# A two-layer graph network: attention steps of three, three and two tiles of keys, each bank of scores with its own tile and activation

## The chip, the cores and the metric

The kernel runs on one core of a Trainium2 chip, as one launch. The metric is the device time of that core in microseconds, as the median of several runs. All data are float32. The core has five engines that run side by side and wait for each other through semaphores: TensorE (PE, matrix products), VectorE (DVE), ScalarE (ACT), GpSimd (POOL) and SyncE (SP, which here only issues DMAs). TensorE writes its results to PSUM, which has eight banks; a bank holds 512 float32 numbers in each of 128 partitions.

## The reference

Sixteen graphs (B) of 1024 nodes (N) with 256 features (C) go through two layers. Layer 0 normalizes, makes queries by a weighted graph product, keys and values by a dense product, and attends with four heads of 64 features. Layer 1 normalizes again, aggregates over the graph and applies two dense products with batch norms. Cut to what bears on the change:

```python
h = jnp.maximum(_layernorm(x), 0.0)
# layer 0
c_adj = jnp.mean(fea, axis=1)                     # fea: h, features first
A = |sigmoid(c_m - c_n) - 0.5| - 0.5, made symmetric, weights adj
g = relu(einsum('bcn,bnm->bcm', fea, Wg) * para)
q = g, split into 4 heads of 64
k, v = (h @ kv_w), split into 4 heads of 64
attn = softmax(einsum('bhnd,bhmd->bhnm', q, k) * scale, axis=-1)
x = x + einsum('bhnm,bhmd->bhnd', attn, v)
# layer 1
h = jnp.maximum(_layernorm(x), 0.0)
agg = einsum('nm,bmd->bnd', A_hat, h)             # A_hat from adj and its degrees
h1 = relu(batchnorm(agg @ W1.T + b1))
x = x + batchnorm(h1 @ W2.T + b2)
```

(The line for `A` and the splits are written out in words here; `...` of the module's other parts are left away.)

## The kernel before, in words

**Units and steps.** Attention is cut into 64 units: a graph b, a pair of heads k (two heads, 128 features together) and a half f of the queries (512 of them). A unit goes over 8 tiles of 128 keys. It is done in steps of two tiles, so four steps a unit, 256 steps in all, 16 a graph. `attention()` (L1215) is the loop over the steps; all instructions of a step are issued in this order:

1. `scores()` (L1043): for each of its tiles, matmuls of keys with queries for both heads (`e`), into a PSUM tile `sc` of two banks, one bank a head; each matmul is split in two halves of 64 keys, so that the four matmuls of a tile lie on four quarters (64*64) of TensorE's array. Then one activation `Exp` on ScalarE over both banks (128 x 1024) makes the tile `p` (L1064). The pool `ps_sc` has two such PSUM tiles, four banks in all; `p` comes from the pool `p4` with four buffers.
2. Actions that were put down for the top or the middle of this step: the sums, the gather and the finish of earlier units.
3. `Unit.add()` (L1079): VectorE adds the step's `p` tiles into `acc`, for the sum over the keys (L1085, L1088).
4. `Unit.values()` (L1091): the values of the step *before*, products of its `p` tiles with v into the bank `o` (L1099, 128*64). After the unit's last step, `o` is transposed in squares to `os` and sent to memory (`out_d`, L1113 and L1117).
5. Pieces of the background, until their cost reaches what is due by this step.
6. Actions for the end of the step: the folds of a finished unit.

**The end of a unit.** Let s be the step in which a unit's last values are taken, which is the first step of the next unit. Its two folds (L1134 and L1135, one for each head: a transpose of `acc` in squares and a reduction to `part`) are issued at the ends of steps s and s+1. `sums` (L1139) stands in the middle of step s+3, right behind that step's scores: matmuls of `part` on TensorE (L1148), then three small VectorE operations that make the reciprocal `inv`. For the first unit of a graph (`opens`; not in graph 0) it is one step later. `gather` reads `os` back at the top of s+2, and `add_output` (L1182) multiplies and adds it to x in step s+4 (s+6 for `opens`).

**The background.** While graph b is attended, the other stages of its neighbours are fed between as pieces of about 1.7 us of TensorE work each: queries (`pg`), keys (`pk`) and values (`pv`) of graph b+1, the aggregation (`pa`) and the hidden layer (`py`) of graph b-1, and the norms and weights of graphs to come. `due` in `attention()` says how much is to be done by each step, evenly over a graph's steps; in the last graph it is bent a little. The products of all these pieces share the pool `ps_mm` of three banks; `o` has one bank, `sc` four, which is all of PSUM.

**Queues.** The schedule is written out by hand (`manual_schedule`): each engine takes its instructions in the order in which this program issues them, and the pools put in the waits for buffers.

**Other names that the change touches.** `rows` and the six columns in `deg` hold sums of the adjacency's rows, diagonals and columns, until graph() and degrees() have made `dinv`. `stats1` collects the statistics for the first batch norm. `csum` are the sums of the normalized features of a node; in `differences()` (L461) VectorE transposes them in squares into `turned`, and SP sends that to memory and reads it back as one row on all partitions (`cbc`), which ScalarE uses to make the weights. In this form `csum` lies in a tile `wide` of 32 columns whose last 24 POOL clears when the norm begins.

After attention of the last graph the second part (`second()`) runs the second dense product with its batch norms; the change does not touch it. A second build of the layers with `shifted_attention` stands behind a condition and is executed only where the first one left the range of the numbers; it is not executed with these inputs.

## Time and profile before

| | us |
|---|---|
| median of 3 runs | 2480.53 |
| lowest and highest | 2480.22, 2481.03 |
| the profiled execution | 2482.2 |
| its span, from the first to the last instruction | 2480.3 |
| TensorE busy | 2418.3 |
| VectorE busy | 1999.8 |
| ScalarE busy | 1261.2 |
| POOL busy | 565.2 |

The mean granted clock of TensorE is 0.992. The profile counts an engine as busy while at least one of its instructions is under way; matmuls overlap each other, so a busy TensorE need not be at its peak. In the lists of groups, a line has the source line, the engine, the operation, the tile written and the tiles read, the size, the count, then the busy time, the mean duration in ns of one, and the idle time of the engine before them with what ended it. In a timeline, a line has the start and the duration of a run of like instructions, and in brackets the idle time before them. PEld are the weight loads of TensorE. A float32 matmul shows as two records, so a step of two tiles has 16 records of scores and 8 of values.

In the steady middle (graphs 2 to 13) every graph repeats the pattern of the one before to within 0.1 us, 16 steps of 7.2 to 9.0 us.

### The profile page before, as it was taken

The page shows a single profiled execution, that of the slowest core. Times are in us where ns is not written, and L with a number is a line of the kernel's source. Part 1 is how long each engine was busy: PE and PEld are TensorE (multiplying, and loading weights), DVE is VectorE, ACT ScalarE, POOL GpSimd, SP SyncE. Part 2 cuts the span into 40 slices and gives each one's busy share as a digit, 9 for nine tenths or more (in the row PEclk, how much of TensorE's full clock was granted, in tenths as well). Part 3 has the DMA queues.
Part 4 walks back from the last instruction along what each step waited for, and adds up shares of the span by engine and source line. Part 5 has one row for each costly group of instructions (what it writes and reads, how often), then busy time and mean ns, then how long its engine had stood idle before and what let it go on. Part 6 is the DMA issues. An engine that isn't in the chain of part 4 may idle for free. (4 is left out here: it accounts for less than half of the span.)

```text
span 2480.3 us, 35952 instructions
## 1 busy us (share of the span) xinstructions
PE 2418.3 (97%) x13290; PEld 829.3 (33%) x13290; DVE 1999.8 (81%) x3103; ACT 1261.2 (51%) x1870; POOL 565.2 (23%) x632
## 2 busy tenths in 40 slices
PE   9999999999999999999999999999999999999995
PEld 4333232332323232323323232323233232334444
DVE  5678887979798888889797978888897978767775
ACT  7764454545463645545454645355454534345554
POOL 1480202112121202021111212120201102136652
PEclk9999999999999999999999999999999999999997
DMA  4665535354555544453545555544535453456559
GB/s 145 198 218 175 181 124 191 120 198 157 181 174 191 168 168 162 144 181 118 210 143 175 170 191 170 187 160 148 177 126 197 133 199 122 157 205 222 192 198 373
DMA packets 202682, 437.19 MB, mean 176 GB/s; under 512 B 21248, under 2 KB 96512, under 8 KB 196736
## 3 DMA queue, kind: packets, MB, share of 16 engines
q1 hardware_dynamic: 173328, 327.29, 39.9%
q0 software_dynamic: 29168, 107.50, 11.4%
q8 instruction: 107, 1.75, 0.3%
q14 instruction: 79, 0.65, 0.1%
HBM read 331.36 MB, written 103.35 MB: 175 GB/s over the span
## 5 line engine op out<-in xcount | busy, mean ns | idle before, releaser
L1064 ACT ACTIVATE p<-sc 128x1024 f32<-128x1024 f32 x512 | 495.6, 1020 | 581.4 <-PE sc L1056 579.7
L1088 DVE TENSOR_TENSOR acc<-acc,p 128x1024 f32<-128x1024 f32 x384 | 469.5, 1223 | 81.6 <-ACT p L1064 60.3
L1056 PE MATMUL sc<-q,k 64*64 64x512 f32 x4096 | 500.1, 603 | 4.2 <-ACT p L1064 4.2
L1099 PE MATMUL o<-p,v 128*64 128x512 f32 x2048 | 494.6, 604 | 0.0
L174 PE MATMUL pa<-aht,h_b 128*64 128x512 f32 x1536 | 346.0, 592 | 1.1 <-ACT h_b L368 1.1
L174 PE MATMUL pg<-w,x_h 128*64 128x512 f32 x1472 | 332.0, 592 | 1.9 <-DVE x_h L579 1.9
L1056 PEld LDWEIGHTS sc<-q,k 64*64 64x64 f32 x4096 | 131.7, 132 | 340.9 <-issue 287.8
L1117 POOL DMA_DIRECT2D out_d<-os x58 | 33.9, 584 | 914.9 <-DVE os L1113 883.9
L1099 PEld LDWEIGHTS o<-p,v 128*64 128x64 f32 x2048 | 124.4, 136 | 297.9 <-issue 272.4
L493 DVE SCALAR_TENSOR_TENSOR w<-w,adj 128x1024 f32<-128x1024 f32 x128 | 166.2, 1306 | 31.9 <-ACT w L514 26.1
L174 PEld LDWEIGHTS pa<-aht,h_b 128*64 128x64 f32 x1536 | 110.0, 137 | 220.7 <-issue 208.8
L174 PEld LDWEIGHTS pg<-w,x_h 128*64 128x64 f32 x1472 | 105.6, 137 | 212.4 <-issue 201.0
L506 ACT ACTIVATE w<-cbc,csum 128x512 f32<-128x512 f32 x256 | 170.3, 716 | 4.7 <-DMA cbc<-csum_d 4.7
L514 ACT ACTIVATE w<-w 128x1024 f32<-128x1024 f32 x128 | 135.5, 1059 | 2.5
L569 DVE TENSOR_TENSOR w<-w,w 128x1024 f32<-128x1024 f32 x112 | 133.2, 1219 | 1.5
L174 PE MATMUL py<-at,w1s 128*64 128x512 f32 x448 | 109.5, 598 | 9.7 <-DVE y L837 7.5
L174 PE MATMUL pv<-kvw_f,ht 128*64 128x256 f32 x1024 | 116.1, 379 | 0.0
L174 PE MATMUL pk<-ht,kvw_f 128*64 128x512 f32 x512 | 115.2, 592 | 0.2 <-ACT ht L430 0.2
L174 PE MATMUL py<-at,w 128*64 128x512 f32 x464 | 113.3, 595 | 1.3 <-DVE at L727 0.7
L368 ACT ACTIVATE x_h<-x_h,lnsm_a 128x256 f32<-128x256 f32 x120 | 70.5, 593 | 74.6 <-DMA aht<-aht_d 67.1
L1085 DVE TENSOR_TENSOR acc<-p,p 128x1024 f32<-128x1024 f32 x64 | 79.2, 1237 | 31.5 <-ACT p L1064 31.5
L1428 ACT ACTIVATE yin_f<-yin_f,sm_f 128x512 f32<-128x512 f32 x128 | 93.5, 802 | 15.0 <-DMA yin_f<-y_d 14.9
(197 smaller groups left out, 2967.1 us busy)
## 6 DMA issues: line engine op xcount, KB each, us to landing
aht<-aht_d SPq DMA_DIRECT2D x224, 512.0 KB
adj<-in_adj_dram SPq DMA_DIRECT2D x128, 512.0 KB
y_d<-y POOLq DMA_DIRECT2D x128, 256.0 KB, 3.8
yin_f<-y_d SPq DMA_DIRECT2D x32, 1024.0 KB
para<-in_para_dram SPq DMA_DIRECT2D x64, 256.0 KB
x_d<-x_x POOLq DMA_DIRECT2D x16, 1024.0 KB, 5.1
xo_f<-x_d SPq DMA_DIRECT2D x32, 512.0 KB
out_dram<-xo_f POOLq DMA_DIRECT2D x32, 512.0 KB, 11.1
```

The lines of the kernel that those rows point to most:

```text
L174: nc.tensor.matmul(dst[r], left[:, r], right, start=start, stop=stop)
L368: nc.scalar.activation(self.h[:, t, :], self.src[:, t, :], AF.Relu, bias=self.sm[:, 1, t : t + 1], scale=self.sm[:, 0, t : t + 1], accum_o ...
L493: nc.vector.scalar_tensor_tensor(w, w, 1.0, a, op0=ALU.add, op1=ALU.mult)
L506: nc.scalar.activation(w[:, t, :].rearrange("p (t q) -> p t q", q=P), cbc[:, q * NT // NH : (q + 1) * NT // NH], AF.Abs, bias=csum[:, th * ...
L514: nc.scalar.activation(made[i], made[i], AF.Tanh, scale=-0.5 / C)
L569: nc.vector.tensor_sub(block(i)[part], block(x)[part], block(y)[part])
L1056: nc.tensor.matmul(sc[part, e, :], ks[b][k][r, m * P + c * HW : m * P + (c + 1) * HW], qs[b][k][r, f * FB : (f + 1) * FB], start=True, sto ...
L1064: nc.scalar.activation(pr, sc, AF.Exp)
L1085: nc.vector.tensor_add(self.acc, self.held, pr)
L1088: nc.vector.tensor_add(self.acc, self.acc, pr)
L1099: nc.tensor.matmul(self.o[r, :], vs[b][k][:, m, r], pr[:, e, :], start=(m == 0), stop=(m == NT - 1),)
L1428: nc.scalar.activation(y, y, AF.Relu, bias=sh[:, j : j + 1], scale=scale[:, j : j + 1])
```

## The change

A step takes three, three and two tiles in place of two each (`GROUPS`), so a unit has three steps. A PSUM tile `sc` has one bank, of which there are four, and each gets an activation of its own (128 x 512). `p` gets six buffers. The sums come one step earlier as counted in steps (s+2, s+3 for `opens`), and the output is added at s+3 (s+5). The work due in the background is counted in tiles instead of steps. To make room, `rows` and five of the degree columns go into a part of `stats1` that is written late, and `csum` gets a tile of 8 columns; `turned` is filled by POOL and transposed in place.

```diff
+        p6 = attn.enter_context(tc.tile_pool(name=f"p6_{kind}", bufs=6, side="right"))
         ps_sc = attn.enter_context(
-            tc.tile_pool(name=f"ps_sc_{kind}", bufs=2, space=PSUM, side="right")
+            tc.tile_pool(name=f"ps_sc_{kind}", bufs=4, space=PSUM, side="right")
         )
...
-        rows = big.tile([P, NH, NT], F32, name="rows")
+        spare = stats1[:, HC - 1].rearrange("p a s -> p (a s)")[:, (B * NH - 10) * 6 :]
+        rows = spare[:, : NH * NT].rearrange("p (q t) -> p q t", t=NT)
...
-        deg_sm = big.tile([P, 6, NT], F32, name="deg")
+        dinv = big.tile([P, NT], F32, name="dinv")
         later = {}
-        row, diag, col, deg, tmp_deg, dinv = (deg_sm[:, i, :] for i in range(6))
+        row, diag, col, deg, tmp_deg = (
+            spare[:, (NH + i) * NT : (NH + i + 1) * NT] for i in range(5)
+        )
...
-                    wide = p2.tile([P, SQ], F32, tag="csum", name=f"csum_{b}")
-                    nc.gpsimd.memset(wide[:, NT:], 0.0)
-                    wides[b] = wide
-                    self.csum = csums[b] = wide[:, :NT]
+                    self.csum = csums[b] = p2.tile([P, NT], F32, tag="csum", name=f"csum_{b}")
...
             turned = p1.tile([P, SQ], F32, tag="csumt", name=f"csumt_{b}")
-            nc.vector.transpose(turned, wides[b])
+            nc.gpsimd.memset(turned[:, NT:], 0.0)
+            nc.gpsimd.tensor_copy(turned[:, :NT], csums[b])
+            nc.vector.transpose(turned, turned)
...
+        GROUPS = (0, 1, 2), (3, 4, 5), (6, 7)
...
-            for m in (2 * g, 2 * g + 1):
-                sc = ps_sc.tile([P, 2, FB], F32, tag="sc", name=f"sc_{b}_{k}_{f}_{m}")
+            for m in GROUPS[g]:
+                pr = p6.tile([P, 2, FB], F32, tag="p", name=f"p_{b}_{k}_{f}_{m}")
                 for e in range(2):
+                    sc = ps_sc.tile([P, FB], F32, tag="sc", name=f"sc_{b}_{k}_{f}_{m}_{e}")
                     r = slice(e * HD, (e + 1) * HD)
                     for c in range(2):
                         part = slice(c * HW, (c + 1) * HW)
                         nc.tensor.matmul(
-                            sc[part, e, :],
+                            sc[part, :],
                             ks[b][k][r, m * P + c * HW : m * P + (c + 1) * HW],
                             qs[b][k][r, f * FB : (f + 1) * FB],
                             start=True,
                             stop=True,
                         )
-                pr = p4.tile([P, 2, FB], F32, tag="p", name=f"p_{b}_{k}_{f}_{m}")
-                nc.scalar.activation(pr, sc, AF.Exp)
+                    nc.scalar.activation(pr[:, e, :], sc, AF.Exp)
                 made.append(pr)
...
-                for i, pr in enumerate(prs):
-                    m = 2 * g + i
+                for m, pr in zip(GROUPS[g], prs):
...
-                if g == NG - 1:
+                if g == len(GROUPS) - 1:
...
             units = [Unit(b, k, f) for b in range(B) for k in range(CC) for f in range(NH)]
+            NG = len(GROUPS)
...
-                    due = total * (s % per_graph + 1) / per_graph
+                    whole = CC * NH * NT
+                    past = (NH * unit.at[1] + unit.at[2]) * NT + GROUPS[g][-1] + 1
+                    due = total * past / whole
                     if b == B - 1:
-                        due -= 0.5 * min(s % per_graph + 1, (per_graph - 1 - s % per_graph) * 0.75)
+                        due -= 0.25 * min(past, (whole - past) * 0.75)
...
                             opens = last.by_squares and last.at[1:] == (0, 0)
-                            wait = 6 if opens else 4
-                            at_mid.setdefault(s + 3 + opens, []).append(last.sums)
+                            wait = 5 if opens else 3
+                            at_mid.setdefault(s + 2 + opens, []).append(last.sums)
```

The changed `shifted_attention` follows the same split into banks; it is not executed.

More of the change, by code (lines that the diff above doesn't have):

```diff
@@ L124, in layers @@
         invs = {}
-        csums, wides, cbcs, weighted, weighers, steps = {}, {}, {}, {}, {}, {}
+        csums, cbcs, weighted, weighers, steps = {}, {}, {}, {}, {}
         s1s = {}
@@ L1006, in shifted_attention @@
                     name = f"{b}_{hd}_{t}"
-                    sc = ps_sc.tile([P, N], F32, tag="sc", name=f"sc_{name}")
+                    scs = [
+                        ps_sc.tile([P, FB], F32, tag="sc", name=f"sc_{name}_{g}") for g in range(NH)
+                    ]
                     for g in range(NH):
                         nc.tensor.matmul(
-                            sc[:, g * FB : (g + 1) * FB],
+                            scs[g],
                             qs[b][k][r, t * P : (t + 1) * P],
@@ L1015, in shifted_attention @@
                         )
-                    sm = p2.tile([P, 3], F32, tag="smx", name=f"smx_{name}")
-                    nc.vector.tensor_reduce(sm[:, 0:1], sc, AX.X, ALU.max, negate=True)
-                    pr = p4.tile([P, N], F32, tag="p", name=f"p_{name}")
-                    nc.scalar.activation(
-                        pr, sc, AF.Exp, bias=sm[:, 0:1], accum_out=sm[:, 1:2]
-                    )
-                    nc.vector.reciprocal(sm[:, 2:3], sm[:, 1:2])
-                    pt = p4.tile([P, N], F32, tag="p", name=f"pt_{name}")
+                    sm = p2.tile([P, 6], F32, tag="smx", name=f"smx_{name}")
+                    for g in range(NH):
+                        nc.vector.tensor_reduce(sm[:, g : g + 1], scs[g], AX.X, ALU.max, negate=True)
+                    nc.vector.tensor_tensor(sm[:, 2:3], sm[:, 0:1], sm[:, 1:2], op=ALU.min)
+                    pr = p6.tile([P, N], F32, tag="p", name=f"p_{name}")
+                    for g in range(NH):
+                        nc.scalar.activation(
+                            pr[:, g * FB : (g + 1) * FB],
+                            scs[g],
+                            AF.Exp,
+                            bias=sm[:, 2:3],
+                            accum_out=sm[:, 3 + g : 4 + g],
+                        )
+                    nc.vector.tensor_add(sm[:, 5:6], sm[:, 3:4], sm[:, 4:5])
+                    nc.vector.reciprocal(sm[:, 2:3], sm[:, 5:6])
+                    pt = p6.tile([P, N], F32, tag="p", name=f"pt_{name}")
                     for g in range(NH):
```

## The prediction

> **What bounds the kernel now.** I read the page's busy table first, then the windows by stage, then the timeline of single attention steps, engine by engine, and last the waits.

> The page:

> ```profile
> span 2480.3 us, 35952 instructions
> PE 2418.3 (97%) x13290; PEld 829.3 (33%) x13290; DVE 1999.8 (81%) x3103; ACT 1261.2 (51%) x1870; POOL 565.2 (23%) x632
> L1064 ACT ACTIVATE p<-sc 128x1024 f32<-128x1024 f32 x512 | 495.6, 1020 | 581.4 <-PE sc L1056 579.7
> L1056 PE MATMUL sc<-q,k 64*64 64x512 f32 x4096 | 500.1, 603 | 4.2 <-ACT p L1064 4.2
> L1099 PE MATMUL o<-p,v 128*64 128x512 f32 x2048 | 494.6, 604 | 0.0
> ```

> TensorE is busy 97%, and in attention (about 54 to 2146 us) it hardly ever waits: 4.2 us in all before score matmuls. So a step costs what TensorE needs to issue it; ScalarE waits for TensorE (579.7 us), not the reverse. One step of TensorE, and its weight loads:

> ```profile
> 1008.45 1.95 PE L1056 MATMUL sc<-q,k 64*64 64x512 f32 x16
> 1010.33 0.31 PE L1148 MATMUL sums<-part,same 128*64 128x32 f32 x4
> 1010.47 1.92 PE L1099 MATMUL o<-p,v 128*64 128x512 f32 x8
> 1012.21 1.89 PE L174 MATMUL pg<-w,s_a 128*64 128x512 f32 x8
> 1013.93 1.89 PE L174 MATMUL pg<-w,x_h 128*64 128x512 f32 x8
> 1015.75 1.52 PE L1056 MATMUL sc<-q,k 64*64 64x512 f32 x12
> ...
> 1008.45 0.21 PEld L1056 LDWEIGHTS sc<-q,k 64*64 64x64 f32 x8 [0.81 <-issue]
> 1008.93 0.15 PEld L1056 LDWEIGHTS sc<-q,k 64*64 64x64 f32 x4 [0.28 <-issue]
> 1009.36 0.15 PEld L1056 LDWEIGHTS sc<-q,k 64*64 64x64 f32 x4 [0.28 <-issue]
> ```

> A tile of keys is 8 score records, in two waves of four side by side; a wave takes 0.429 us (the weight loads of the third wave come 0.43 after those of the second; the products from 1012.21 to 1015.75 are eight waves and one change of kind). The step from 1008.45 to 1015.75 is 7.30 us: 16 waves are 6.86, the sums 0.14, and 0.30 are left over. They lie where the array changes between 64*64 and 128*64 and in each kind's first wave.

> The start of attention shows the one place where two steps of scores follow each other with nothing between:

> ```profile
> 54.13 1.95 PE L1056 MATMUL sc<-q,k 64*64 64x512 f32 x16
> 56.57 2.00 PE L1056 MATMUL sc<-q,k 64*64 64x512 f32 x16 [0.49 <-ACT p L1064]
> ...
> 55.51 1.92 ACT L1064 ACTIVATE p<-sc 128x1024 f32<-128x1024 f32 x2
> ...
> 1009.61 1.94 ACT L1064 ACTIVATE p<-sc 128x1024 f32<-128x1024 f32 x2 [2.10 <-PE sc L1056]
> ```

> The third tile there waits until the first tile's activation (55.51 + 1.02) has emptied its banks. An activation that waits only for TensorE starts 1.16 us after its step (1009.61 against 1008.45).

> Last, VectorE around the second fold of a unit, in a step that starts at 1065.84:

> ```profile
> 1065.84 1.95 PE L1056 MATMUL sc<-q,k 64*64 64x512 f32 x16
> ...
> 1067.75 0.70 DVE L1134 STREAM_TRANSPOSE acc<-acc 128x512 f32<-128x512 f32 x1
> 1068.49 0.69 DVE L1135 TENSOR_REDUCE part<-acc 128x16 f32<-128x512 f32 x1
> ```

> The fold belongs to the end of the step before, and yet ends at 1069.18, 3.34 us into this one: VectorE runs that far behind TensorE. From the same times for every unit: in graphs 2 to 13 the second fold ends 6.6 us into step s+2 for a graph's first unit and 3.1 to 3.3 us for the other three (s is the step in which the unit's last values are taken). The sums today come one step later still, so nobody feels this.

> [...] last score wave to first values wave is 0.52 us instead of 0.43, the same into the scores. [...] here a tile's scores take 0.86 us and its activation 1.02. [...] so a score matmul that waits holds the values behind it; the 0.49 us at 56.57 is such a wait. [...] The trace's copies of 512 elements from PSUM take 585, and I use 585.

> **The change part by part.** The profiled run took 2482.2 us around its span of 2480.3; the median is 2480.5. Sums are made against the run, and 1.7 comes off at the end.

> (a) Steps go from 4 to 3 a unit, 64 units: 64 steps fewer, 0.30 each: **-19 us**. Matmuls, adds and background pieces keep their numbers.

> (b) The third tile of a step. There are four one-bank tiles for six banks of scores, so tile 3 takes the banks of tile 1 of the same step. Let a step start at 0. Tile 1's activations start at 1.15; the first head's ends at 1.73; the second starts 0.485 later (585 less the 0.10 overlap of today's pairs: 1.02 long, 0.92 apart), at 1.63, and ends at 2.22; 0.04 later (56.53 to 56.57) TensorE may go on, at 2.26. It would have come to tile 3 at 0.48 + 3 x 0.429 = 1.77. The first head is just in time, the second 0.49 late[...]. Two steps of three: 128 x 0.49 = **+63 us**. It is a new wait on TensorE; queued behind it are the values and the whole background of the step.

> (c) ScalarE late at such a step. Today the first activation of a step is later than 1.16 by 3.9 us a graph, unfelt: 0.7 at tile 2, 2.6 at tile 4, 0.5 at tile 14 in a steady graph (behind the tanh work of L506 and L514). The step that starts at tile 3 lies between the first two, about 1.7, and there it now stops TensorE in full. 14 graphs x 1.8 = **+25 us**; at least 0 (if the longer step lets ScalarE catch up), at most 3.9 x 14 = 55.

> (d) The sums come at s+2 instead of s+3 (s+3 for the first unit of a graph, from graph 1 on). For the other 48 units step s+2 is a unit's third, of two tiles: TensorE gets to the sums 1.87 us after its start, while `part` comes from the fold emitted at the end of s+1. With today's lag (1.0 to 4.6, graphs 0 and 15 included) TensorE waits 1.37 in the mean: 48 x 1.37 = **+66 us**. Behind this wait stand values and background again. Bounds: fold alone is 1.39 after the last background result, so 0.3 at least (+14); going through VectorE's list of a three-tile step by hand (three adds 3.9, weighing or hidden work up to 9, fold 1.4, against a step of 12.8 to 14) I get 2.6, 4.2 and 4.7 for the three units, mean wait 2.0 (+96).

> (e) At no cost: 1024 activations for 512 (0.97 us a tile instead of 0.92, 26 us in all on an engine that is half idle; beyond (b) and (c) covered by values and background). Six `p` buffers for three a step: still reused after two steps. The due times keep their totals. `rows` and the degree columns only move. The copy and memset of 8 and 24 columns on POOL in front of the transpose of the column sums: 15 times, some 0.5 us of VectorE wait each by POOL's small steps; the row is needed a step later (ScalarE's wait for it is 4.7 us in all today); if that cover fails, +7. The gather of `os` stays at s+2 and its use moves from s+4 to s+3, a step of 9 us or more away; it stands on SP behind the same loads as now, and if late it holds VectorE only.

> Sum: -19 + 63 + 25 + 66 = +135; 2482.2 + 135 - 1.7 = **2615 us**.

> **The rivals.**
> - Only the banks stop TensorE (b, c), the sums are in time because the 12.8 us step gives VectorE slack: 2480.5 + 69 = 2550. For it: VectorE is at 81%. Against it: the lag is made of work that follows the last background product, not of a backlog.
> - VectorE falls further behind in long steps: waits of 2.9 us at the sums (139), and the hidden stage, whose products wait for VectorE today already (7.5 us in all), loses 10 more: 2480.5 - 19 + 63 + 25 + 139 + 10 = 2698. For it: the hand count of 4.2 and 4.7. Against it: each stop of TensorE lets VectorE catch up.
> - Faster: tile 3 finds its banks empty, as one-bank activations are meant to allow, and (a) alone is left: 2461. It is one mechanism, the release of tile 1's second bank: it decides from a stall below 19/128 = 0.15 us a step, so the release would have to come at 1.92 instead of 2.26, and the fold within 1.9 us of its step. For it: the first head does fit (1.77). Against it: two activations in a row end no sooner than 1.15 + 1.07 by the trace.

> **How the numbers follow.** Forecast 0.61; sums in time 0.17; VectorE behind 0.15; faster 0.06; about equal 0.01. The range 2535 to 2690 takes in most of the second and third cases: (a) and (b) alone give 2524, the upper bounds of (c) and (d) 2675. About 0.2% is what a measurement of this kernel can tell from no change. Slower holds all but the last two cases: 0.93.

> **What would show it.** (a) right if the page has 192 steps with some 0.30 us left over each. (b) right if weight loads of scores wait for the activation some 128 times, and values follow 3.2 us after the start of a three-tile step and not 2.7; wrong if 2.7. (c): in each graph one such wait near 2 us. (d) right if the weight loads of the sums wait for the reduce, about 48 times by 1 to 2 us. TensorE's share should fall to some 94%, not more, since in (b) the first head's matmuls still run and count as busy. If TensorE's busy time falls with the steps and neither wait shows, I am wrong and it is faster.

## The result, and the profile after

| | before | after |
|---|---|---|
| median, us (4 runs each, side by side) | 2480.78 | 2701.72 |
| lowest and highest | 2480.22, 2484.66 | 2700.52, 2703.07 |
| after / before, 95% interval | | 1.0887 (1.0868 to 1.0906) |
| span of the profiled execution | 2480.3 | 2698.3 |
| mean granted TensorE clock | 0.992 | 0.974 |

The changed kernel is 221 us slower. The direction is the one forecast. The size is not: 2701.72 lies 87 us above the forecast of 2615 and outside its range. The page of the kernel after: busy times, two rows of the slices, and four groups.

```profile
span 2698.3 us, 36449 instructions
PE 2512.9 (93%) x13290; PEld 876.0 (32%) x13290; DVE 2012.9 (75%) x3103; ACT 1287.0 (48%) x2382; POOL 561.7 (21%) x646
...
PE   9958989899999999898999999998989999999995
...
PEclk9979999999999999999999999999999999999997
...
L1078 ACT ACTIVATE p<-sc 128x512 f32<-128x512 f32 x1024 | 520.9, 609 | 499.3 <-PE sc L1071 499.2
L1071 PE MATMUL sc<-q,k 64*64 64x512 f32 x4096 | 561.2, 606 | 42.1 <-ACT p L1078 41.8
L1112 PE MATMUL o<-p,v 128*64 128x512 f32 x2048 | 514.7, 636 | 0.0
...
L1161 PE MATMUL sums<-part,same 128*64 128x32 f32 x256 | 20.4, 236 | 92.6 <-DVE part L1148 92.6
```

TensorE, the bound before, has the same 13290 records and yet 94.6 us more of busy time (2512.9 against 2418.3): its matmuls wait with some of their tiles started, or run slower. The third slice (135 to 202 us) falls to 5 tenths, which no step of the forecast had foreseen. The waits of TensorE itself:

```profile
PE sums L1161 <- DVE part L1148: 92.6, 46, 6.1
PE sc L1071 <- ACT p L1078: 41.8, 18, 25.6
```

(total, times, longest.) The sums wait for the reduction of the fold 46 times. The scores wait only 18 times by this view, and 25.6 us of it is one wait; what the third tiles wait is hidden here, since the first head's matmuls still count as busy. The weight loads show it, in a three-tile step of the kernel after that starts at 1146.75:

```profile
1146.75 0.21 PEld L1071 LDWEIGHTS sc<-q,k 64*64 64x64 f32 x8 [0.81 <-issue]
1147.24 0.15 PEld L1071 LDWEIGHTS sc<-q,k 64*64 64x64 f32 x4 [0.28 <-issue]
1147.67 0.15 PEld L1071 LDWEIGHTS sc<-q,k 64*64 64x64 f32 x4 [0.28 <-issue]
1148.53 0.20 PEld L1071 LDWEIGHTS sc<-q,k 64*64 64x64 f32 x4 [0.71 <-ACT p L1078]
1149.01 0.19 PEld L1071 LDWEIGHTS sc<-q,k 64*64 64x64 f32 x4 [0.29 <-ACT p L1078]
1150.02 0.20 PEld L1112 LDWEIGHTS o<-p,v 128*64 128x64 f32 x4 [0.81 <-DVE acc L1147]
```

The third tile's first head goes 1.77 us after the step's start and its second head at 2.26, both to the hundredth as forecast. The values follow at 3.27 us; without a wait it would be 2.72 (two waves after 1.77, the second of them with the change of kind: 0.43 + 0.52).

A timeline of TensorE at the sums, in a step that starts at 1122.40:

```profile
1122.40 1.95 PE L1071 MATMUL sc<-q,k 64*64 64x512 f32 x16
1127.16 0.43 PE L1161 MATMUL sums<-part,same 128*64 128x32 f32 x4 [2.82 <-DVE part L1148]
1127.37 4.02 PE L1112 MATMUL o<-p,v 128*64 128x512 f32 x12
```

The sums begin 4.76 us into a two-tile step, not 1.87. The 12 records of values behind them take 4.02 us, where six waves of 0.43 should need some 2.8. The windows of the same place say why (start and end, length, busy time of each engine with its instructions, then the granted clock, the DMA share and GB/s):

```profile
1117.00:1123.00 6.00, 6.00 (x34) 1.91 (x34) 4.37 (x5) 5.57 (x8) 0.00 (x0) 1.00 0.00 1
1126.50:1129.90 3.40, 2.74 (x10) 1.08 (x12) 2.61 (x6) 0.00 (x0) 0.00 (x0) 0.50 0.27 77
1130.00:1136.00 6.00, 6.00 (x36) 2.01 (x36) 3.60 (x4) 0.12 (x1) 0.00 (x0) 1.00 0.01 3
```

TensorE was granted half its clock for 3.4 us, beginning towards the end of the stop. The record of the clock has 22 spells of half clock in attention, 102.4 us in all (27.3 of it in the long stop shown next); in attention the kernel before has one, of 3.4 us. Twenty of the 22 last 3.413 us, one 6.827 and one 27.307; from 240 us on, the stops of TensorE at the sums with a spell last 2.5 to 3.2 us.

Last, the one long stop, in graph 0 (timeline of several engines):

```profile
170.72 0.58 POOL L299 DMA_DIRECT2D aht_d<-one  x1
...
173.40 0.18 POOL L467 COPY csumt<-csum 128x8 f32<-128x8 f32 x1
173.62 0.21 DVE L468 STREAM_TRANSPOSE csumt<-csumt 128x32 f32<-128x32 f32 x1 [27.20 <-POOL csumt L467]
...
179.79 1.33 ACT L509 ACTIVATE w<-cbc,csum 128x512 f32<-128x512 f32 x2 [25.20 <-DMA cbc<-csum_d]
...
183.15 2.46 PE L1071 MATMUL sc<-q,k 64*64 64x512 f32 x8 [25.65 <-ACT p L1078]
```

Read upwards, TensorE waited 25.65 us for an activation of scores, which stood on ScalarE behind the weights, which waited for the row `cbc`, which VectorE had not transposed because it had waited 27.20 us for a copy of 0.18 us on POOL. That copy stood behind graph()'s work on the adjacency (the issue at 170.72 is its last here) and two small operations of degrees(); POOL took them in the order of issue, without a pause from 141 us on.

By graphs, the length between starts against the kernel before: graph 0 +33.1, graph 1 +16.0, graphs 2 to 13 +11.9 to +14.3, graph 14 +9.8, graph 15 +6.8; the parts ahead of and behind attention are equal within 0.3.

### The profile page after: what moved, and what is told of

Read it like the earlier page. It is cut to its first block, busy times and chain, and to the rows that moved or that the text cites. A ratio compares the mean times of both kernels' runs of the same rounds, so it can differ in the third digit from the quotient of the medians.

```text
span 2698.3 us, 36449 instructions
## 1 busy us (share of the span) xinstructions
PE 2512.9 (93%) x13290; PEld 876.0 (32%) x13290; DVE 2012.9 (75%) x3103; ACT 1287.0 (48%) x2382; POOL 561.7 (21%) x646
## 5 line engine op out<-in xcount | busy, mean ns | idle before, releaser
L1078 ACT ACTIVATE p<-sc 128x512 f32<-128x512 f32 x1024 | 520.9, 609 | 499.3 <-PE sc L1071 499.2
L1071 PE MATMUL sc<-q,k 64*64 64x512 f32 x4096 | 561.2, 606 | 42.1 <-ACT p L1078 41.8
L1112 PE MATMUL o<-p,v 128*64 128x512 f32 x2048 | 514.7, 636 | 0.0
L1071 PEld LDWEIGHTS sc<-q,k 64*64 64x64 f32 x4096 | 148.9, 132 | 427.1 <-issue 215.7
L1112 PEld LDWEIGHTS o<-p,v 128*64 128x64 f32 x2048 | 142.3, 143 | 297.3 <-issue 273.4
L496 DVE SCALAR_TENSOR_TENSOR w<-w,adj 128x1024 f32<-128x1024 f32 x128 | 159.8, 1249 | 69.1 <-ACT w L517 64.6
L369 ACT ACTIVATE h_b<-x_x,lnsm_b 128x256 f32<-128x256 f32 x128 | 69.9, 601 | 98.2 <-DVE lnsm_b L358 98.2
L1161 PE MATMUL sums<-part,same 128*64 128x32 f32 x256 | 20.4, 236 | 92.6 <-DVE part L1148 92.6
```

The source lines that it names most:

```text
L369: nc.scalar.activation(self.h[:, t, :], self.src[:, t, :], AF.Relu, bias=self.sm[:, 1, t : t + 1], scale=self.sm[:, 0, t : t + 1], accum_o ...
L496: nc.vector.scalar_tensor_tensor(w, w, 1.0, a, op0=ALU.add, op1=ALU.mult)
L1071: nc.tensor.matmul(sc[part, :], ks[b][k][r, m * P + c * HW : m * P + (c + 1) * HW], qs[b][k][r, f * FB : (f + 1) * FB], start=True, stop=True,
L1078: nc.scalar.activation(pr[:, e, :], sc, AF.Exp)
L1112: nc.tensor.matmul(self.o[r, :], vs[b][k][:, m, r], pr[:, e, :], start=(m == 0), stop=(m == NT - 1),)
```

## The experiments

Ten kernels, one question each. "Before" is always the kernel before, run beside it.

| | median, us | before, us | ratio (95%) |
|---|---|---|---|
| e1_csum_dve | 2676.77 | 2483.73 | 1.0789 (1.0766 to 1.0813) |
| e2_sums_later | 2618.11 | 2483.73 | 1.0549 (1.0526 to 1.0571) |
| e3_both | 2592.06 | 2483.73 | 1.0449 (1.0427 to 1.0472) |
| e4_pairs | 2589.46 | 2483.73 | 1.0432 (1.0410 to 1.0454) |
| e5_split_only | 2484.33 | 2483.91 | 1.0000 (0.9992 to 1.0009) |
| e6_csum_pool | 2506.38 | 2483.91 | 1.0096 (1.0079 to 1.0112) |
| e7_five | 2564.5 | 2483.91 | 1.0332 (1.0315 to 1.0350) |
| e8_two_mm | 2507.45 | 2483.91 | 1.0102 (1.0085 to 1.0118) |
| e9_sums_early | 2533.73 | 2482.56 | 1.0206 (1.0189 to 1.0223) |
| e10_filled | 2647.11 | 2483.34 | 1.0662 (1.0645 to 1.0680) |

**The copy on POOL.** Undone in the kernel after (e1), and put alone into the kernel before (e6).

```diff
-            nc.gpsimd.memset(turned[:, NT:], 0.0)
-            nc.gpsimd.tensor_copy(turned[:, :NT], csums[b])
+            nc.vector.memset(turned[:, NT:], 0.0)
+            nc.vector.tensor_copy(turned[:, :NT], csums[b])
```

> The changed kernel with one part undone: VectorE instead of POOL clears and copies the column sums ahead of their transpose. Theory (POOL's queue): the 26 us stop in graph 0 goes, and with it one spell of halved TensorE clock, so about 2670 us (2665 to 2678). Rival (third tile): VectorE would be late there anyhow and the stop only moves to another wait; over 2690 us.

> The kernel before with one part of the change alone: POOL clears and copies the column sums ahead of the transpose. Theory (POOL's queue): VectorE stops in graph 0 behind POOL's work on the adjacency, TensorE after it, 20 to 30 us, about 2506 us. Rival (hidden, as forecast): within 7 us of before.

Measured: -25 us in the one, +22.5 in the other, both as expected. In e6 graph 0 is 27.0 us longer and graph 1 2.2 shorter; it is one wait of TensorE's in graph 0:

```profile
PE sc L1055 <- ACT p L1063: 30.3, 2, 29.8
```

So two operations of a fifth of a microsecond cost 22 to 25 us, through the queue they stand in. In graphs 1 to 15 they cost nothing that the totals show.

**The time of the sums.** In the kernel after, at s+3 for all units but the last two (a graph's first unit, from graph 1 on, stood there already; e2), and the same with the copy on VectorE (e3).

```diff
+                            late = opens or last.index < UNITS - 2
-                            wait = 5 if opens else 3
-                            at_mid.setdefault(s + 2 + opens, []).append(last.sums)
+                            wait = 5 if opens else 3 + late
+                            at_mid.setdefault(s + 2 + late, []).append(last.sums)
```

> The changed kernel with the sums at s+3 for every unit (output at s+4; only the last unit but one stays at s+2). Theory (sums too early): the 93 us of TensorE idle before the sums go, and with them most of the 20-odd half-clock windows of 3.4 us in attention (some 37 us): about 2575 us (2560 to 2595), with under 5 us idle before the sums. Rival (third tile): VectorE's lag only stops TensorE elsewhere; over 2650 us.

> Both of the above. Theory: the two add up, about 2545 us (2530 to 2560); what is left over the kernel before is the third tile's wait, 128 times some 0.6 us, plus late activations at two steps a graph, less 19 us for 64 fewer steps: 60 to 75 us. Rival (third tile is all): not under 2640 us.

Measured: -84 us for e2 and -110 for e3 against the kernel after; the expectations were missed by 43 and 47. The two parts do add up (-25 and -84 make -109). The mechanism did what was expected of it: one wait of 1.0 us is left before the sums, and the mean granted clock rises from 0.974 to 0.990 in e3. But part of the time reappears. The waits of TensorE in e3:

```profile
PE sc L1071 <- ACT p L1078: 28.6, 32, 4.7
PE pa L175 <- ACT h_b L369: 8.5, 2, 7.5
PE py L175 <- DVE y L864: 8.4, 13, 0.7
PE py L175 <- DVE y L841: 7.4, 12, 0.6
PE py L175 <- DVE y L846: 4.8, 12, 1.6
```

In the kernel after, `py` waited for VectorE's `y` 3.5 us in all, the scores 16 without the long stop, and `pa` 1.1. With the sums out of the way TensorE meets VectorE and ScalarE at other places, and VectorE no longer gets the pauses in which it caught up. This is read from lists of waits; no run isolates it. A graph in the steady middle of e3 is 6.2 us longer than before. Its third tiles account for that much: eight steps whose values follow 0.55 to 1.56 us late, 6.2 in sum (1.56 and 1.17 where ScalarE is late as well), and the four steps saved (-1.2) cancel against the longer waits of `py`.

**The half clock.** The kernel of e1, with two products of constants (1.72 us of TensorE) in front of the sums of a graph's third and fourth unit. They go into the bank that the sums then overwrite, so the values are released no earlier.

```diff
+                whole = bank(f"sums_{self.name}")
+                if b > 0 and self.index % (CC * NH) >= 2:
+                    for _ in range(2):
+                        product(whole, ident, later["w1"][:, 0, :FB], True, True)
-                pt = bank(f"sums_{self.name}")[:, : 2 * J * NS]
+                pt = whole[:, : 2 * J * NS]
```

> This is the kernel after the change with the column sums copied on VectorE (2677 us), and in graphs 1 to 15 two products of constants (8 records of 512 columns, four waves of 0.43 = 1.72 us) are issued into the bank of the sums right before the sums of a graph's third and fourth unit, which are the two that stop TensorE for some 2.9 us. They leave out nothing; the sums overwrite them. Values are released at the same moment as without them, so as waits they change nothing: 92.5 - 32 x 1.72 = about 37 us of idle time before the sums. Theory A (the spells of halved TensorE clock that follow these stops lengthen the kernel): the stops are cut to 1.2 us, which by the run of the kernel before with early sums is too short for a spell; 21 spells of 78.5 us in all become about three; one that starts 0.7 us before a stop ends costs (3.41 - 0.7) / 2 = 1.4 us, so 18 x 1.4 = 25 us come back: 2652 us, and between 2640 and 2660. Rival B (VectorE sets the pace in these steps, so that a slow TensorE is hidden): the spells go and the time stays at 2677. Rival C (spells come for another reason than these stops): the spells stay, and the time is 2677 to 2685, longer by the changes of tile at the added products.

Measured: 2647.11, which is 29.7 us less than e1, for work that does nothing. Theory A holds. The timeline of TensorE at such a stop in e1, then in e10:

```profile
1097.88 1.95 PE L1071 MATMUL sc<-q,k 64*64 64x512 f32 x16
1102.64 0.43 PE L1161 MATMUL sums<-part,same 128*64 128x32 f32 x4 [2.82 <-DVE part L1148]
1102.85 4.09 PE L1112 MATMUL o<-p,v 128*64 128x512 f32 x12
```

```profile
1086.20 1.95 PE L1071 MATMUL sc<-q,k 64*64 64x512 f32 x16
1088.07 1.94 PE L175 MATMUL sums<-w,ident 128*64 128x512 f32 x8
1090.87 0.31 PE L1165 MATMUL sums<-part,same 128*64 128x32 f32 x4 [0.86 <-DVE part L1148]
1091.01 2.77 PE L1112 MATMUL o<-p,v 128*64 128x512 f32 x12
```

The sums come at nearly the same moment, 4.76 and 4.67 us into the step; the values behind them take 4.09 us in the one and 2.77 in the other. The mean granted clock is 0.979 in e1 and 0.990 in e10, and in e10 it is 1.00 over the time from 947.3 to 1094.6 us, where the kernel after has one spell and 0.99. The kernel after shows the price of a spell as well: of its graphs 3 to 13, those with two spells take 148.9 to 149.2 us and those with one 147.4 to 147.5.

```profile
1085.50:1088.92 3.42, 1.44 (x11) 0.70 (x13) 2.83 (x7) 0.28 (x1) 0.00 (x0) 1.00 0.98 317
1088.92:1092.33 3.41, 3.41 (x18) 1.37 (x16) 2.92 (x4) 0.14 (x1) 0.06 (x1) 1.00 0.33 72
1123.05:1126.46 3.41, 1.29 (x13) 0.15 (x4) 3.34 (x6) 2.72 (x6) 0.00 (x0) 1.00 0.00 0
1126.46:1129.87 3.41, 2.71 (x10) 1.08 (x12) 2.62 (x6) 0.00 (x0) 0.00 (x0) 0.50 0.27 77
```

An edge of the raster cuts the longer stop, TensorE is busy for 42% of the stretch (1.44 of 3.42), and the clock stays. The shorter one leaves it 38% (1.29 of 3.41), and half clock follows. In attention these two traces have 1257 such stretches at full clock: all 22 in which TensorE was busy, as the profile counts it, for 39% or less were followed by half clock, and of the 1235 others, all at 42% or more, one was (56%, in graph 0). With 1.72 us of products in a stop of 2.94 us 1.22 are left, so by an estimate from these numbers TensorE is busy for some 64% of a stretch (2.19 of 3.413) even where the whole rest of the stop falls into it.

**Which kind of step.** In e3, the scores in pairs of banks again, one activation of 1024 for both heads (e4); and two-tile steps with the one-bank tiles and activations left as they are (e5).

```diff
+                sc = ps_sc.tile([P, 2, FB], F32, tag="sc", name=f"sc_{b}_{k}_{f}_{m}")
...
-                    nc.scalar.activation(pr[:, e, :], sc, AF.Exp)
+                nc.scalar.activation(pr, sc, AF.Exp)
```

```diff
-        GROUPS = (0, 1, 2), (3, 4, 5), (6, 7)
+        GROUPS = (0, 1), (2, 3), (4, 5), (6, 7)
...
-                            wait = 5 if opens else 3
-                            at_mid.setdefault(s + 2 + opens, []).append(last.sums)
+                            wait = 6 if opens else 4
+                            at_mid.setdefault(s + 3 + opens, []).append(last.sums)
```

> As the run with both, but the scores go back to two tiles of two banks and one activation of 1024 (steps of three, three and two stay). Theory: the third tile then waits for one activation of 1.02 us, 1.16 + 1.02 + 0.04 = 2.22 against 1.77, so 0.45 for both heads, no longer than with one bank each: within 15 us of the run with both, rather below. Rival (the split shortens the wait): slower than it by over 20 us. Rival (twice the activations are what costs): faster than it by over 40 us.

> The changed kernel with steps of two tiles again (four a unit, sums at s+3, s+4 for a graph's first unit, output at s+4 and s+6, as before) and the column sums on VectorE; each bank keeps its own tile and activation. Theory (the third tile, not the split, costs): as the kernel before within 8 us, about 2482; no score waits for an activation. Rival (1024 activations or one-bank tiles cost by themselves): over 2520 us.

Both came as expected. Splitting the activation costs nothing in two-tile steps (ratio 1.0000, 12 and 15 runs) and gains nothing in three-tile steps (2592.06 against 2589.46). In e4 the wait becomes visible on TensorE itself, since both heads of a third tile now stand still:

```profile
PE sc L1071 <- ACT p L1078: 72.1, 128, 4.6
```

128 is two third tiles for each of the 64 units, and 72.1 / 128 = 0.56 us each.

**A fifth bank.** e3 with five banks of scores. The bank comes from the products (`ps_mm` 2 in place of 3), so the queries are made one feature half after the other and the idle products at the start go into the bank of `o`. e8 is the kernel before with these adaptations alone, to price them.

```diff
-            tc.tile_pool(name=f"ps_sc_{kind}", bufs=4, space=PSUM, side="right")
+            tc.tile_pool(name=f"ps_sc_{kind}", bufs=5, space=PSUM, side="right")
...
-        ps_mm = st.enter_context(tc.tile_pool(name=f"ps_mm_{kind}", bufs=3, space=PSUM))
+        ps_mm = st.enter_context(tc.tile_pool(name=f"ps_mm_{kind}", bufs=2, space=PSUM))
```

> Three, three and two tiles with the sums at s+3 and the column sums on VectorE, but five banks for scores and two for all other products (the queries of graphs 0 and 1 made one feature half after the other, the idle matmuls of the start in the bank of the values). Theory (third tile waits for the second bank of the first): its first head finds a free bank and its second the one that is released at 1.77 us, just when it comes, so values follow 2.75 us after the start of a step instead of 3.3, and 128 x 0.55 = 70 us go: 2522 us, plus what two banks cost the other products (the next run measures that). Rival (ScalarE's pace, not the banks, holds the third tile): 3.3 us stay and the time is over 2590.

> A control: the kernel before with two banks instead of three for the products outside the attention's own, with the same two adaptations. No theory of the change speaks on it; between 2481 and 2540 us, and its distance from before is what the five-bank run pays for its bank.

Measured: in six of a steady graph's eight three-tile steps the values follow 2.78 to 2.84 us after the start instead of 3.27 to 3.33 (time of the sums taken off), and in the other two, where ScalarE is late, they too come some 0.49 earlier. So it is the missing fifth bank that holds them. The time falls by 28 us to 2564.5, and with the expected 70 and e8's +23.5 it should have been 2545 or less: 19 us are missed. Some 11 of these were never there to gain: in the 126 steps that can be compared the values come 59.5 us earlier in sum, not 70. The waits show a part of the rest:

```profile
PE py L175 <- DVE y L864: 24.2, 13, 1.9
PE sc L1071 <- ACT p L1078: 8.8, 5, 3.3
```

This wait of the hidden layer for VectorE has grown from 8.4 to 24.2 us, and with its two like ones from 20.6 to 34.2, while the scores' own fell from 28.6 to 8.8. Why the two banks of products and the longer steps add up to more than each alone was not settled.

**Sums early in short steps.** The kernel before, with nothing changed but the sums at s+2.

```diff
-                            at_mid.setdefault(s + 3 + opens, []).append(last.sums)
+                            at_mid.setdefault(s + 2 + opens, []).append(last.sums)
```

> The kernel before with one thing changed: the sums one step earlier (s+2, and s+3 for a graph's first unit), as the change has them; steps of two tiles and all else stay. Theory A (the price as forecast, the lag less 1.87 us): 48 waits of 1.4 us in the mean, TensorE idle before the sums about 65 us, and stops that short leave the clock alone: about 2548 us. Theory B (any stop before the sums also halves the clock for 3.4 us): 45 half-clock windows more, about 2625 us. Theory C (TensorE's stop is given back elsewhere, since VectorE catches up): under 2520 us.

Measured: +51 us, nearest to A. The waits of TensorE:

```profile
PE sums L1148 <- DVE part L1135: 42.1, 31, 2.7
PE sums L1148 <- ACT p L1064: 16.8, 13, 1.3
```

The second line belongs to the fold as well: in each of these stops the reduction ends 0.05 to 0.15 us before the sums begin. In a steady graph the sums begin 1.52, 1.36 and 1.47 us later in their steps than in the kernel before (4.35), and the graph grows by 3.57, so about a fifth is given back. The mean granted clock is 0.992, that of the kernel before: the stops of e9, 1.34 us in the mean, leave no mark on it.

## Why the forecast was right in direction and too small

By its own steps, with the change of span (+218.0 us) as the whole:

| step | forecast | measured | from |
|---|---|---|---|
| (a) 64 fewer steps | -19 | about -19 | step of e3 |
| (b) third tile waits for the second bank | +63 | +73 | 128 x 0.57 |
| (c) ScalarE late | +25 | +32 | steps of after |
| (d) sums wait for the fold | +66 | +92.6 | waits of after |
| (e) copy on POOL | 0 (7 if uncovered) | +25 | e1, e6 (+22.5) |
| half clock after the stops | not foreseen | +30 | e10 against e1 |
| sum | +135 | +234 | |

The measured column is taken from waits and from differences of runs, and overlaps: it sums to 16 us more than the whole. Waits are partly given back later, as e9 shows, where the graph grew by a fifth less than its stops.

(a) A two-tile step without sums in e3 takes 8.04 us for 18 waves (7.72), so 0.32 is left over, as priced. The saving itself was not isolated.

(b) Right, mechanism and moment. The stall is 0.55 to 0.61 instead of 0.49. The records of the first wave after a restart take 640 ns instead of 589, which is the first 0.06, and in half of the steps the activations begin 0.06 later (1.18 instead of 1.12). The price of an activation was not the error: over all 1024 the mean is 609 ns, but the two that free the banks of the first tile take 593 and 591, near the 585 that I used. e4 and e7 show the cause: 128 waits, and with a fifth bank at most 0.12 us of this kind is left in a step.

(c) About right in sum, which is partly luck, since it was not right in place. Over all 128 three-tile steps of the profile after, without the one that stops for 25.65 us, the values follow 105 us later than 2.72 us after the start; (b) is 73 of it and 32 are left. The step that starts at tile 3 loses 0.99 a graph, not 1.8; the steady graphs lose 1.2 in all, and about 14 us lie in graphs 0 and 1, which the forecast left out.

(d) This step failed. The text took "today's lag" for the fold, a mean wait of 1.37 in 48 steps, and put the count through VectorE's list (lags of 2.6, 4.2 and 4.7, mean wait 2.0) only into the bound. The steps show lags of 2.2, 4.7 and 4.6, and the mean wait is 92.6 / 46 = 2.0. That count was right in the mean and should have been the forecast, since the lag belongs to the length of the step and to what the step puts in front of the fold. In the kernel after, in front of the fold that the stop at 1124 waits for (timeline of VectorE):

```profile
1123.25 0.69 DVE L583 TENSOR_TENSOR x_h<-x_h 128x512 f32<-128x512 f32 x1
1123.86 1.22 DVE L496 SCALAR_TENSOR_TENSOR w<-w,adj 128x1024 f32<-128x1024 f32 x1
1124.99 0.68 DVE L559 TENSOR_TENSOR q<-q,para 128x512 f32<-128x512 f32 x1
1125.59 0.70 DVE L1147 STREAM_TRANSPOSE acc<-acc 128x512 f32<-128x512 f32 x1
1126.33 0.69 DVE L1148 TENSOR_REDUCE part<-acc 128x16 f32<-128x512 f32 x1
```

Background work of the long step stands there, without a pause, until 3.2 us after the next step has begun. The lag of the short steps predicts short steps well: in e9 TensorE stops 44 times before the sums, 58.9 us in all or 1.34 each, where the text had 1.37. It was only the wrong lag for the new ones.

(e) This step failed too. It costed the copy "by POOL's small steps", from the durations, with a cover of one step. It left out what is ahead of the copy on POOL in graph 0, which is the queue that had to be counted. The rest of (e) stands: e5 shows split activations, six buffers, the due times and the moved rows together at 0.4 us. The earlier use of `os` is not in e5; VectorE's list of waits in the kernel after has none for the gather.

The half clock was no step at all. TensorE's clock was taken as constant though the forecast itself made stops of up to 2.7 us (a lag of 4.6 less 1.87). Rival "VectorE further behind" (2698) came within 4 us of the time, partly by luck, since only part of its reasons held: the waits at the sums that it put at 139 are 92.6, and the rest is the copy and the clock.

What stays open: some 8 of the 19 us of e7, and how much of what e2 and e3 fell short by belongs to each of the waits that grew. No run with three-tile steps came below the kernel before, and e5, which equals it, has none; so a faster version was not found.

## What to carry to other kernels

When steps are made longer, everything that was timed in steps has to be counted anew through each engine's list for the new step; a lag measured in the old one is not a property of the work. An instruction that is put on another engine costs what stands ahead of it in that engine's queue at that moment, in the worst stage and not in the steady one: here a copy of 0.18 us came after 27.20 us of waiting. And a stop of the bounding engine can have a price behind it as well, here 3.4 us at half clock behind stops of 2.8 us: look at the granted clock of the next few microseconds before pricing a wait at its own length.

## What the hardware showed that was not expected

- The length of the stops counted here, not their sum alone. In e9 TensorE stopped 44 times before the sums, 58.9 us in all, and in its timeline from 1000 to 1150 us the stops last 1.29 to 1.45 us; the mean granted clock was the 0.992 of the kernel before. In the kernel after there are 46 such waits, 92.6 us in all, two a steady graph of 2.8 us or more; one or two spells of half clock, of 3.41 us each, follow in each steady graph, and the mean granted clock was 0.974.
- Not every such stop brings one. In the traces of the kernels before and after the changes of clock lie on a raster of 3.413 us; 39% busy or less in a stretch of it was followed by half clock in 22 of 22 cases, 42% and more in 1 of 1235. With 1.72 us of products in such a stop (e10) the mean granted clock rose from 0.979 to 0.990.
- A product that does nothing was worth its time here: 240 records of 592 ns, put where TensorE stood still anyway, made the kernel 29.7 us faster.
